# A state-space scan on one core: six of 24 products with B move to ScalarE, and all exponentials go to SBUF

## The chip, the core and the metric

The kernel runs on one core of a Trainium2 chip. The metric is device time in microseconds (us) of one execution, as the median of several runs. A profiled execution gives the trace from which every duration below comes. Engines are named as the profile names them: PE is TensorE (PEld its weight loads), DVE VectorE, ACT ScalarE, POOL GpSimd, SP SyncE, which issues the DMAs.

## What is computed

The kernel computes a small network of four layers. Only layer 0 is touched by the change. It is two Mamba blocks one after the other on a tensor of 4 batches, 96 channels and 4096 tokens, then a mix of channels and a batch normalization. One block, cut to what matters (a state of 16 numbers is kept for each of 192 inner channels):

```
h = layernorm(seq); xs, z = split(h @ in_w)          # 192 channels each
xc = silu(causal convolution of xs with 4 taps + conv_b)
dt, Bm, Cm = split(xc @ xproj_w)                      # 6, 16 and 16 columns
delta = softplus(dt @ dt_w + dt_b)
dA  = exp(delta[..., None] * A)                       # channels x 16 states
dBx = delta[..., None] * Bm[:, :, None, :] * xc[..., None]
state[t] = dA[t] * state[t-1] + dBx[t]
y = sum over states of state[t] * Cm[t] + Dp * xc
out = (y * silu(z)) @ out_w
```

The remaining layers (a convolution block, a linear attention, two feed-forward blocks in 8-bit floats and a mix by Fourier transforms) follow from about 2540 us.

## The kernel before

**Items and tiles.** The tokens of a batch are cut into four sections of T = 1024. An item is one section of one batch in one of the two blocks: 4 x 4 x 2 = 32 items, done one after the other, four batches between two sections of the same batch. An item has 192 channels x 16 states = 3072 rows of tokens, laid out as 24 tiles of 128 partitions x 1024 tokens. A tile is (p, g, j): p is a third of the channels (64), j a half of that third (32), g a group of four states; the partitions are 4 states x 32 channels. The tiles of an item stand in `order`, and the whole program is written out by hand in steps: step m is tile m % 24 of item m // 24, and each engine's queue holds its instructions in the order in which the steps issue them. A *slot* is a step counted from an item's own start.

**The work of one tile.** The exponential dA = exp(delta x A) is made on ScalarE (`exp`, L488) from delta, which was copied to all four state groups of partitions by DMA (`ddb`). The product u = (delta x xc) x B needs B's row on each state's 32 partitions. For 14 of the 24 tiles TensorE spreads B into PSUM with a selecting matrix (`rep`, L474, one for both halves j where they share it), and VectorE multiplies it with `udb` (delta x xc, also copied by DMA) (L523). For the other ten (`pool_tiles`) GpSimd multiplies `udb` by `brep`, B's rows copied by DMA (`times_b`, L509 for two tiles at once, L511 for one). VectorE then scans the 1024 tokens (`scan`, L529). GpSimd multiplies two scanned tiles by C (`times_c`, L534, 128 x 2048), in place in `hs`. TensorE adds up the states (`sum_y`, L551) into a PSUM bank `y`, which starts with Dp x xc (`start_y`, L544). VectorE multiplies by silu(z) (`gate`, L562).

**Where operands lie.** For VectorE's tiles dA is `da` in SBUF and u is in PSUM; the incoming state is put into the first column of `da` by ScalarE (`enter`, L497), and the scan starts from 1.0. For GpSimd's tiles dA is `dap` in PSUM (tag u) and u is `up` in SBUF; the scan takes the state by a pointer. [...] `AHEAD` = 3 is how many tiles ahead an exponential is made and the number of `da` buffers; `hs` has five buffers.

**The first stage.** The steps of an item's preparation (`first_stage`) run up to two items ahead of its scans, each at a given slot (`at_slot`): load x, the layer norm (L282 to L329, with `nt` in the tag up2), the four-tap convolution (`spread`, L215), silu with its table loads (L350), x-projection (L229), softplus (L377), delta and delta x xc to HBM (`spread_out`) and back to all partitions (`load_d`, `load_u`), B and C rows (`load_b`, `load_c`). ScalarE copies most results out of PSUM (L339, L369). Before the first item `prepare` makes the weights; there the convolution taps come by a DMA that broadcasts one row to 97 partitions (L167) and are multiplied with the input weights on VectorE (L184).

Of the kernel before, what the change touches and what calls it, by code (L numbers as in the profile page):

```python
# [9 lines left out]
F32 = mybir.dt.float32  # L10
# [40 lines left out]
class Net:  # L51
# [43 lines left out]
    def layer0(self, dram, scratch):  # L95
        tc, nc, ins = self.tc, self.nc, self.ins
        x_in = ins["x"]
        with ExitStack() as ctx:
# [3 lines left out]
            psum_y = ctx.enter_context(tc.tile_pool(name="l0y", bufs=2, space=PSUM))  # L102
# [44 lines left out]
            AHEAD = 3  # L147
# [3 lines left out]
            def load_weights():  # L151
                for name, shape in (
                    ("sel_r", [128, 32]),
                    ("sel_b", [64, 4, 128]),
# [8 lines left out]
            def prepare():  # L163
                with tc.tile_pool(name="l0s", bufs=1) as wk, tc.tile_pool(name="l0g", bufs=1) as sums_pool:
                    in_w = load(wk, "in_w", [C, 2, HID])
                    rows = wk.tile([C + 1, 2, 4, DIN], F32, name="conv_taps")
                    nc.sync.dma_start(rows, ins["conv_rows"].partition_broadcast(C + 1))  # L167
# [5 lines left out]
                    nc.vector.tensor_scalar_mul(nega, nega, -1.0)  # L173

# [14 lines left out]

                    layer(0)  # L190

                    for m in sorted(stages[0])[:4]:
                        for f in stages[0].pop(m):
                            f()
                    layer(1)
# [14 lines left out]
            def spread(ws, rhs, p):  # L210

                ps = tile_ps(128)
# [48 lines left out]
            def first_stage(k):  # L261
# [16 lines left out]
                @at_slot(-9)  # L278
# [11 lines left out]
                @at_slot(-8)  # L290
                def _():
                    if k:
                        nt = wk.tile([128, 2, T + 1], F32, name="nt", tag="up2")[:, 0]
                    else:
                        nt = first_pool.tile([128, 8 * C], F32, name="nt")
# [12 lines left out]
                @at_slot(-7)  # L308
# [5 lines left out]
                @at_slot(-6)  # L314
# [7 lines left out]
                @at_slot(-5)  # L322
# [10 lines left out]
                def parts_of(name, ws, rhs, slots, bufs):  # L333
# [7 lines left out]
                    for p, (t, out) in enumerate(slots):  # L341
                        at_slot(t)(lambda p=p: m.update({(name, p): spread(ws, rhs, p)}))
                        at_slot(out)(lambda p=p: into(p, m[name, p]))


                parts_of("xc", [(w_x[:, i, k], k) for k in range(4)], n, ((-4, -2), (-3, 0), (-1, 1)), 2)

                @at_slot(2)
# [25 lines left out]

                @at_slot(9)
                def _():
                    nc.scalar.activation(m["delta"], m["delta"], AF.Softplus)  # L377
                    exp_set()
# [18 lines left out]
                parts_of("z", [(w_z[:, i], 3)], n, ((12, 13), (12, 13), (13, 14)), 2)  # L397

                for p in range(3):
                    for j in range(2):  # L400
                        at_slot((15, 23, 31)[p] + j)(lambda p=p, j=j: load_d(m, p, j))
                    at_slot((16 if k else 15, 23, 31)[p])(lambda p=p: load_u(m, p))
                for g, t in ((0, 21), (1, 24), (3, 25), (2, 27)):
                    at_slot(t)(lambda g=g: load_c(m, g))
                at_slot(17 if k else 6)(lambda: load_b(m, 3))
                at_slot(22)(lambda: load_b(m, 2))
# [40 lines left out]
            outer = [(0, 0), (0, 1), (3, 0), (1, 0), (1, 1), (3, 1), (2, 0), (2, 1)]  # L447
            inner = [(0, 0), (3, 0), (0, 1), (3, 1), (1, 0), (2, 0), (1, 1), (2, 1)]
            order = [(p, g, j) for p, eight in enumerate((outer, inner, outer)) for g, j in eight]
            pool_tiles = (2, 5, 7, 9, 11, 13, 15, 18, 21, 23)  # L450
            group_starts = (0, 3, 6, 8, 10, 12, 14, 16, 19, 22)
            ends = {max(t for t, x in enumerate(order) if x[:2] == (p, g)): (p, g) for p in range(3) for g in range(4)}
            sums = {5: (0, 0), 8: (0, 1), 9: (0, 3), 12: (0, 2), 14: (1, 0), 16: (1, 3)}
            sums |= {18: (1, 1), 19: (1, 2), 23: (2, 0), 24: (2, 1), 26: (2, 3), 27: (2, 2)}
            starts = {3: 0, 13: 1, 17: 2}
            gates = {13: 0, 21: 1, 29: 2}
            NTL = len(order)
            last = len(items) * NTL

            def on_pool(m):  # L460
                return m % NTL in pool_tiles
# [5 lines left out]
            def rep(m):  # L467

                k, t = divmod(m, NTL)
                x = psum_x.tile([128, T], F32, name="rep", tag="x")  # L470

                for q, at in enumerate(halves):
                    rows = slice(32 * q, 32 * q + 32)
                    nc.tensor.matmul(  # L474
                        x[:, at], sel_b[rows, order[t][1]], made[k]["dbl"][rows, at], start=True, stop=True
# [1057 lines left out]
```

## Time and profile before

| what | value |
|---|---|
| device time, median of 3 runs | 3846.45 us (3835.75 to 3846.96) |
| the profiled execution's own time | 3837.67 us |
| its span, first to last instruction | 3835.5 us |
| first scan of layer 0 starts, last ends | 78.9 and 2527.7 us |
| scans / products with B on DVE / on POOL, in tiles of an item | 24 / 14 / 10 |
| scan L529 (da, rep) and (dap, state, up), mean | 2288 and 2325 ns |
| product L523 on DVE, mean | 1214 ns |
| products on POOL: with C L534, with B L509 | 4186 and 4533 ns |
| exponential L488 on ACT, mean | 1115 (to PSUM), 1144 ns (to SBUF) |

How to read the views: the busy share counts time in which an engine executes, averaged over the span; 40 slices show it over time in tenths. A group's line gives line, engine, operation, out<-in with shapes, count, then busy us, mean ns of one, and the idle time in front of it with the engine that ended it. A timeline's row gives start, duration, engine, line, operation and count; consecutive instructions overlap a little, so costs in a row are best taken from start to start.

### The profile page before, as it was taken

The page shows a single profiled execution, that of the slowest core. Times are in us where ns is not written, and L with a number is a line of the kernel's source. Part 1 is how long each engine was busy: PE and PEld are TensorE (multiplying, and loading weights), DVE is VectorE, ACT ScalarE, POOL GpSimd, SP SyncE. Part 2 cuts the span into 40 slices and gives each one's busy share as a digit, 9 for nine tenths or more (in the row PEclk, how much of TensorE's full clock was granted, in tenths as well). Part 3 has the DMA queues.
Part 4 walks back from the last instruction along what each step waited for, and adds up shares of the span by engine and source line. Part 5 has one row for each costly group of instructions (what it writes and reads, how often), then busy time and mean ns, then how long its engine had stood idle before and what let it go on. Part 6 is the DMA issues. An engine that isn't in the chain of part 4 may idle for free. (4 is left out here: it accounts for less than half of the span.)

```text
span 3835.5 us, 43134 instructions
## 1 busy us (share of the span) xinstructions
PE 3238.0 (84%) x13656; PEld 1305.1 (34%) x13656; DVE 3036.5 (79%) x2704; ACT 2387.5 (62%) x4640; POOL 2836.6 (74%) x922
## 2 busy tenths in 40 slices
PE   6888888888888888888888888756799998999888
PEld 2222222222222222222222222126544534766643
DVE  4999999999999899999999999962573384444649
ACT  4666676666667666776666666541345686656557
POOL 1999999999999999999999999932001064444527
PEclk9888888887888778887878778757899999999989
DMA  7656666666676566666666666556200000011101
GB/s 182 167 154 165 165 165 165 165 161 154 165 172 164 145 165 163 160 157 165 157 154 169 161 158 163 151 135 211 77 1 1 1 1 6 18 37 35 36 9 58
DMA packets 177867, 463.82 MB, mean 121 GB/s; under 512 B 50804, under 2 KB 52734, under 8 KB 174304
## 3 DMA queue, kind: packets, MB, share of 16 engines
q1 hardware_dynamic: 177640, 461.08, 47.3%
q8 instruction: 108, 1.77, 0.2%
q14 instruction: 119, 0.97, 0.1%
HBM read 387.40 MB, written 73.50 MB: 120 GB/s over the span
## 5 line engine op out<-in xcount | busy, mean ns | idle before, releaser
L534 POOL TENSOR_TENSOR hs<-hs,crep 128x2048 f32<-128x2048 f32 x384 | 1595.8, 4186 | 30.8 <-DVE hs L529 27.0
L474 PE MATMUL rep<-dbl,sel_b 32*128 32x512 f32 x1280 | 458.7, 794 | 365.6 <-DVE hs L529 364.4
L529 DVE TENSOR_TENSOR_SCAN hs<-da,rep 128x1024 f32<-128x1024 f32 x320 | 732.1, 2288 | 35.1 <-ACT da L488 0.7
L488 ACT ACTIVATE dap<-ddb,nega 128x1024 f32<-128x1024 f32 x320 | 356.9, 1115 | 491.8 <-DVE hs L529 490.9
L509 POOL TENSOR_TENSOR up<-udb,brep 128x2048 f32<-128x2048 f32 x128 | 580.3, 4533 | 84.0 <-DMA ddb<-dd 82.8
L488 ACT ACTIVATE da<-ddb,nega 128x1024 f32<-128x1024 f32 x448 | 512.4, 1144 | 76.6 <-DVE hs L529 71.9
L529 DVE TENSOR_TENSOR_SCAN hs<-dap,state,up 128x1024 f32<-128x1024 f32 x240 | 558.1, 2325 | 0.0
L551 PE MATMUL y<-hs,sel_r 128*32 128x512 f32 x3072 | 522.5, 768 | 16.8 <-POOL hs L534 16.7
L523 DVE TENSOR_TENSOR rep<-udb,rep 128x1024 f32<-128x1024 f32 x320 | 388.5, 1214 | 71.2 <-PE rep L474 71.1
L215 PE MATMUL ps<-n,w_x 97*64 97x512 f32 x1536 | 367.2, 621 | 0.0
L474 PEld LDWEIGHTS rep<-dbl,sel_b 32*128 32x128 f32 x1280 | 120.5, 218 | 672.9 <-issue 547.4
L529 DVE TENSOR_TENSOR_SCAN hs<-da,u 128x1024 f32<-128x1024 f32 x128 | 293.0, 2289 | 12.6 <-DVE u L523 0.5
L1091 POOL CAST hq<-y 128x1536 fp8e5<-128x1536 f16 x64 | 93.9, 1467 | 218.8 <-issue 122.6
L215 PEld LDWEIGHTS ps<-n,w_x 97*64 97x64 f32 x1536 | 110.6, 141 | 254.8 <-issue 196.7
L551 PEld LDWEIGHTS y<-hs,sel_r 128*32 128x32 f32 x3072 | 71.9, 122 | 359.9 <-issue 266.9
L529 DVE TENSOR_TENSOR_SCAN hs<-dap,up 128x1024 f32<-128x1024 f32 x80 | 181.3, 2266 | 1.8 <-ACT dap L488 1.7
L523 DVE TENSOR_TENSOR u<-udb,rep 128x1024 f32<-128x1024 f32 x128 | 157.4, 1229 | 25.4 <-DMA udb<-ud 11.9
L965 POOL MEMSET h<- 1x4096 f32 x1 | 3.5, 3506 | 212.9 <-DVE n L871 212.9
L1230 POOL TENSOR_TENSOR av<-av,ec 128x780 f32<-128x780 f32 x32 | 58.7, 1836 | 133.7 <-ACT av L1227 133.7
L511 POOL TENSOR_TENSOR up<-udb,brep 128x1024 f32<-128x1024 f32 x64 | 151.6, 2369 | 0.0
L544 PE MATMUL y<-xc,dp 128*128 128x512 f32 x192 | 140.6, 821 | 0.0
L1203 POOL TENSOR_TENSOR f<-p,p 128x390 f32<-128x390 f32 x64 | 65.1, 1038 | 95.0 <-DVE p L1195 95.0
(260 smaller groups left out, 5962.0 us busy)
## 6 DMA issues: line engine op xcount, KB each, us to landing
ddb<-dd SPq DMA_DIRECT2D x768, 128.0 KB
udb<-ud SPq DMA_DIRECT2D x768, 128.0 KB
crep<-cd SPq DMA_DIRECT2D x512, 128.0 KB
brep<-cd SPq DMA_DIRECT2D x256, 128.0 KB
dd<-delta SPq DMA_DIRECT2D x64, 384.0 KB
band<-in_band SPq DMA_DIRECT2D x24, 1024.0 KB
ud<-delta SPq DMA_DIRECT2D x62, 384.0 KB
x<-in_x SPq DMA_DIRECT2D x32, 384.0 KB
```

The lines of the kernel that those rows point to most:

```text
L215: nc.tensor.matmul(ps[rows], w[:, 64 * p : 64 * p + 64], rhs[:, at.start + shift : at.stop + shift], start=k == 0, stop=k == len(ws) - 1, ...
L474: nc.tensor.matmul(x[:, at], sel_b[rows, order[t][1]], made[k]["dbl"][rows, at], start=True, stop=True)
L488: nc.scalar.activation(da, made[k]["dd", h, j], AF.Exp, scale=nega[:, col : col + 1])
L509: nc.gpsimd.tensor_mul(up, u, twice(made[k]["brep", g]))
L511: nc.gpsimd.tensor_mul(up[:, js[0]], u[:, js[0]], made[k]["brep", g])
L523: nc.vector.tensor_mul(u, made[k]["ud", h][:, j], x)
L529: nc.vector.tensor_tensor_scan(hs[:, 1:], made[k].pop(("da", t)), u, st, ALU.mult, ALU.add)
L534: nc.gpsimd.tensor_mul(hs[:, :, :T], hs[:, :, 1:], twice(made[k]["crep", g]))
L544: nc.tensor.matmul(y, dp[:, items[k][2], p], made[k]["xc"][:, p], start=True, stop=True)
L551: nc.tensor.matmul(made[k]["y", p][row : row + 32], sel_r, made[k]["hs", p, g][:, j, at], start=False, stop=True, skip_group_check=True,)
L1091: nc.gpsimd.tensor_copy(q, y2, saturate=False)
L1203: nc.gpsimd.tensor_add(f[i][:, r], pp[0][:, :, r, :], pp[1][:, :, 1 - r, :])
```

## The change

In layer 0, of an item's 24 products with B, VectorE does 12 (groups g = 0 and 1), GpSimd 6 (`GP` = 2) and ScalarE 6 (`GA` = 3). For ScalarE's six, tokens lie on partitions: TensorE transposes B (`tb`, slot 8) and delta x xc (`turn_du`, slots 15 to 17) into a y bank, ScalarE copies both out (`bt`, `keep_du`), multiplies each of 8 blocks of 128 tokens by each of 4 states' B, which is now a scale per partition (`weigh`, 32 instructions of 128 x 192, slots 19 to 28), and TensorE transposes the result into PSUM, eight transposes a tile (`fill`). Every exponential is written to `da` in SBUF, four ahead with four buffers; `enter` is gone, and every scan takes its state by a pointer. The tiles stand in pairs of the same p and g. PSUM tags x and u are filled in turn. `hs` has four buffers and serves `nt` too; the two y banks have tags of their own and take a third of z, and the transposes of du and B. Slots move by one or so. In `prepare`, the taps come as one row and are spread by three matmuls. The diff, cut to its core:

```diff
-            AHEAD = 3
+            AHEAD = 4
+            GP, GA = 2, 3
...
-                    rows = wk.tile([C + 1, 2, 4, DIN], F32, name="conv_taps")
-                    nc.sync.dma_start(rows, ins["conv_rows"].partition_broadcast(C + 1))
+                    row = load(wk, "conv_rows", [1, 2 * 4 * DIN])
...
+                    def spread_taps(q):
+                        at = slice(q * MB, (q + 1) * MB)
+                        ps = wide(C + 1, MB, q)
+                        nc.tensor.matmul(ps, one, row[:, at], start=True, stop=True)
+                        nc.vector.tensor_copy(taps[:, at], ps)
...
+            def y_bank(k):
+                return psum_y.tile([128, MB], F32, name="y", tag=f"y{k % 2}")
...
-                        nt = wk.tile([128, 2, T + 1], F32, name="nt", tag="up2")[:, 0]
+                        nt = wk.tile([128, 2, T + 1], F32, name="hs", tag="hs", bufs=4)[:, 0]
...
+                @at_slot(8)
+                def _():
+                    m["tb"] = y_bank(3 * k - 2)[:, : 8 * 2 * NST].rearrange("p (q s) -> p q s", q=8)
+                    for q in range(8):
+                        nc.tensor.transpose(
+                            m["tb"][:, q], dbl[: 2 * NST, q * 128 : q * 128 + 128], self.ident[: 2 * NST, : 2 * NST]
+                        )
...
+                    m["bt"] = cp.tile([128, 8, 4], F32, name="bt", tag="bt", bufs=2)
+                    nc.scalar.copy(m["bt"], m["tb"][:, :, 4 * GA : 4 * GA + 4])
...
-                parts_of("z", [(w_z[:, i], 3)], n, ((12, 13), (12, 13), (13, 14)), 2)
+                parts_of("z", [(w_z[:, i], 3)], n, ((12, 13), (12, 13), (14, 15)), 2, 3 * k - 3)
+
+                def turn_du(p):
+                    ps = m["ut", p] = y_bank(3 * k - 3)
+                    for a in range(4):
+                        at = slice(a * 128, a * 128 + 128)
+                        nc.tensor.transpose(ps[:, at], m["du"][:, p, at], self.ident)
...
+                for p in range(3):
+                    at_slot(16 + p)(lambda p=p: keep_du(p))
+                    at_slot(15 + p)(lambda p=p: turn_du(p))
+
+                def weigh(of):
...
+                    for e in of:
+                        q, s4 = divmod(e, 4)
+                        nc.scalar.mul(
+                            m["uta"][:, q, :, 32 * s4 : 32 * s4 + 32].rearrange("t (p j) d -> t p j d", p=3),
+                            m["udt"][:, :, q].rearrange("t p (j d) -> t p j d", j=2),
+                            m["bt"][:, q, s4 : s4 + 1],
+                        )
+
+                e = 0
+                for t, count in ((19, 4), (20, 2), (21, 2), (22, 5), (23, 5), (24, 5), (26, 1), (27, 2), (28, 6)):
+                    at_slot(t)(lambda of=range(e, e + count): weigh(of))
+                    e += count
...
-            outer = [(0, 0), (0, 1), (3, 0), (1, 0), (1, 1), (3, 1), (2, 0), (2, 1)]
-            inner = [(0, 0), (3, 0), (0, 1), (3, 1), (1, 0), (2, 0), (1, 1), (2, 1)]
-            order = [(p, g, j) for p, eight in enumerate((outer, inner, outer)) for g, j in eight]
-            pool_tiles = (2, 5, 7, 9, 11, 13, 15, 18, 21, 23)
+            order = [(p, g, j) for p, gs in enumerate(((0, 2, 1, 3), (0, 2, 3, 1), (3, 0, 2, 1))) for g in gs for j in range(2)]
+            fills = {3: 4, 5: 6, 6: 7, 7: 8, 10: 12, 11: 13, 13: 14, 15: 16, 16: 17, 17: 18, 19: 22, 23: 24}
...
+            def fill(m):
...
+                tag = "xu"[len(filled) % 2]
+                x = psum_x.tile([128, T], F32, name="rep", tag=tag)
+                filled[m] = x, tag
+                if g == GA:
+                    for q in range(8):
+                        nc.tensor.transpose(x[:, q * 128 : q * 128 + 128], made[k]["uta"][:, q, 2 * h + j], self.ident)
+                    return
...
-                if on_pool(m):
-                    da = psum_x.tile([128, T], F32, name="dap", tag="u")
-                else:
-                    da = wk.tile([128, T], F32, name="da", tag="da", bufs=AHEAD)
-                made[k]["da", t] = da
+                da = made[k]["da", t] = wk.tile([128, T], F32, name="da", tag="da", bufs=AHEAD)
                 nc.scalar.activation(da, made[k]["dd", h, j], AF.Exp, scale=nega[:, col : col + 1])
-
-            def enter(m):
...
-                    nc.scalar.mul(a0, a0, state[:, b, i, col : col + 1])
...
+                up = made[k]["up", p] = wk.tile([128, 2, T], F32, name="up", tag="up")
+                nc.gpsimd.tensor_mul(up, made[k]["ud", p], twice(made[k]["brep", GP]))
...
+                if g == GP:
+                    u = made[k]["up", h][:, j]
+                elif g == GA:
+                    u, _ = filled[m]
                 else:
 
-                    u = x if on_pool(m + 1) else psum_x.tile([128, T], F32, name="u", tag="u")
+                    x, tag = filled[m - j]
+                    u = x if j else psum_x.tile([128, T], F32, name="u", tag="u" if tag == "x" else "x")
                     nc.vector.tensor_mul(u, made[k]["ud", h][:, j], x)
...
-                st = 0.0 if s == 0 else state[:, b, i, col : col + 1] if on_pool(m) else 1.0
+                st = state[:, b, i, col : col + 1] if s else 0.0
                 nc.vector.tensor_tensor_scan(hs[:, 1:], made[k].pop(("da", t)), u, st, ALU.mult, ALU.add)
...
-            b_slots = {3: [(0, 1, 3, (0, 1))], 4: [(0, 0, 2, (1,))], 9: [(0, 1, 2, (0, 1))], 13: [(0, 2, 3, (0, 1))]}
-            b_slots[20] = [(0, 2, 2, (1,)), (1, 0, 3, (0, 1))]
+            b_slots = {5: (0, 1), 15: (0, 2), 23: (1, 0)}
```

## The prediction

> **What bounds the kernel now.** I read the page's busy shares and its 40 slices first, then the groups, then the timelines of single engines in layer 0. The last chain on the page lies in the later layers, which the change leaves alone; I don't use it.
>
> ```profile
> PE 3238.0 (84%) x13656; PEld 1305.1 (34%) x13656; DVE 3036.5 (79%) x2704; ACT 2387.5 (62%) x4640; POOL 2836.6 (74%) x922
> ...
> DVE  4999999999999899999999999962573384444649
> ACT  4666676666667666776666666541345686656557
> POOL 1999999999999999999999999932001064444527
> ```
>
> Layer 0 is the first 26 slices. In it VectorE and GpSimd both stand at 9, ScalarE at 6. The groups' view puts the first scan at 78.9 us and the last at 2525.4 (ending 2527.7), for 32 items: 2448.8/32 = 76.5 us an item.
>
> ```profile
> core 0: us, PE busy (x) PEld busy (x) DVE busy (x) ACT busy (x) POOL busy (x), PEclk, DMA share, GB/s
> 1000.00:1400.00 400.00, 343.72 (x1390) 101.44 (x1388) 380.24 (x216) 277.07 (x542) 396.23 (x101) 0.82 0.65 161
> ```
>
> In the middle of layer 0 GpSimd is busy 99%, VectorE 95%, TensorE 86%, ScalarE 69%. So two engines bound it together.
>
> ```profile
> L534 POOL TENSOR_TENSOR hs<-hs,crep 128x2048 f32<-128x2048 f32 x384 | 1595.8, 4186 | 30.8 <-DVE hs L529 27.0
> ...
> L529 DVE TENSOR_TENSOR_SCAN hs<-da,rep 128x1024 f32<-128x1024 f32 x320 | 732.1, 2288 | 35.1 <-ACT da L488 0.7
> ...
> L529 DVE TENSOR_TENSOR_SCAN hs<-dap,state,up 128x1024 f32<-128x1024 f32 x240 | 558.1, 2325 | 0.0
> ...
> L523 DVE TENSOR_TENSOR rep<-udb,rep 128x1024 f32<-128x1024 f32 x320 | 388.5, 1214 | 71.2 <-PE rep L474 71.1
> ```
>
> The operands matter. A scan reads either da (SBUF) and rep or u (PSUM), or dap (PSUM) and up (SBUF); a product reads udb (SBUF) and rep (PSUM). No large VectorE instruction of layer 0 has two SBUF inputs (the one L394 of the first item apart).
>
> ```profile
> 1500.88 2.29 DVE L529 TENSOR_TENSOR_SCAN hs<-da,rep 128x1024 f32<-128x1024 f32 x1
> 1503.09 2.33 DVE L529 TENSOR_TENSOR_SCAN hs<-dap,state,up 128x1024 f32<-128x1024 f32 x1
> 1505.50 1.23 DVE L523 TENSOR_TENSOR u<-udb,rep 128x1024 f32<-128x1024 f32 x1
> 1506.84 2.29 DVE L529 TENSOR_TENSOR_SCAN hs<-da,u 128x1024 f32<-128x1024 f32 x1
> ```
>
> From start to start: scan 2.20 us, scan with a state pointer 2.24 (2.41 where the next product waits for its bank), product 1.33, gate 0.6. An item is 14x2.20 + 10x2.24 + 14x1.33 + 3x0.6 = 73.6 us; the rest of the 76.5 is waiting, most of it for rep: 71.1+1.7 us in all, 2.3 an item.
>
> [...] a later layer has such a pair:
>
> ```profile
> 3559.08 0.55 DVE L1242 SCALAR_TENSOR_TENSOR zz<-av 128x384 f32<-128x384 f32 x1
> ...
> 3559.30 2.43 POOL L1203 TENSOR_TENSOR f<-p,p 128x390 f32<-128x390 f32 x2 [3.44 <-DVE p L1195]
> 3559.54 0.85 DVE L1245 SCALAR_TENSOR_TENSOR z<-av 128x6 f32<-128x6 f32 x1
> ...
> 3560.32 0.55 DVE L1242 SCALAR_TENSOR_TENSOR zz<-av 128x384 f32<-128x384 f32 x1
> 3560.78 0.98 DVE L1245 SCALAR_TENSOR_TENSOR z<-av 128x6 f32<-128x6 f32 x1
> ```
>
> L1245 handles 6 elements and takes 0.15 us alone; here 0.85 and 0.98, each ending just as a GpSimd product (about 0.93) ends. The two GpSimd instructions take 2.43 together instead of 1.86. With both queued, the two engines alternate.
>
> [...] here eight transposes at L318 take 1.30 us, 0.16 each[...].
>
> **The change, part by part (an item, layer 0).**
>
> *VectorE's own work.* Two products fewer: -2x1.33 = -2.7. All scans take the state by pointer: 14x0.04 x 3/4 of the items = +0.4. Net -2.3.
>
> *Exponentials in SBUF.* Six scans an item (B group 2, tiles 2, 3, 10, 11, 20, 21) now read da and up, both in SBUF. The trace has no such scan; I bound it. Below: nothing[...]. Above: a full GpSimd instruction ahead of every one of the six, 6x4.15 = 25. I take the alternation shown above. In VectorE's queue the two scans of a pair follow one another; in GpSimd's the product with C of the pair before (L534, 4.15 from start to start) becomes ready when the scan before this pair ends. So the first scan issues at once, that product waits for it (2.24), runs, and the second scan waits for the product: 4.15 for each of three pairs, 12.4 us. Is GpSimd free when the first scan comes? Its work is 12x4.15 + 3x4.49 + 3.40 = 66.7, and 6x2.24 = 13.4 of being shut out makes 80.1; below the period that comes out, so mostly yes. Behind the waiting scan stand all later scans and products; behind them ScalarE's exponentials (four ahead) and TensorE's fills.
>
> *GpSimd.* It loses one pair and two single products with B: 4.5+2x2.35 = 9.2. In the program before that would count; now it hides behind VectorE.
>
> *ScalarE.* 32 weighings of 192 elements. Eight at L312 with 96 elements take 1.80 us from start to start, 0.225 each[...] I take 0.31: 9.9 us, with three copies of 512 at 0.49 (start to start in ScalarE's timeline) and a small one, 11.5. Away go 14 one-element products (L497, 0.19) in three quarters of the items, 2.0. ScalarE rises from some 53 (69% of 76.5) to 62 us, hidden beside VectorE's 88, and still if VectorE stood at its own 72.
>
> *TensorE.* Six fills become eight transposes each; ten broadcasts become six: 6x(1.3 to 1.7) - 4x1.1; twelve transposes of du 1.9, eight of B 0.8: about +7, to 72 us. Hidden in sum, not in order. Where a new wait sits: at slot 15 the first transpose of du needs the y bank that ScalarE's copy of z empties, and that copy stands behind the exponential which needs scan 15's buffer. After scan 15: 1.05 + 0.49 + 0.65 for the transposes + 1.5 for tile 17's fill + about 0.2 of signals = 3.9, while scan 16 covers 2.24: VectorE waits 1.7. The next fill stands behind a transpose that needs the copy at slot 16, which has the squares of the norm (2.4) and an exponential before it: another 1.6. Together 3.3, of which I count as new only what exceeds the 2.3 waited for rep before, which the earlier fills can remove: +1.0, between 0 and +3.3.
>
> *Moved.* The norm's nt takes a turn of hs, whose buffers go from five to four; at four, scan 16 waits for the product with C of tiles 10 and 11; VectorE's tiles 12 to 15 lie between (2x2.24 + 2x3.57 = 11.6), and GpSimd needs 3.4+4.15. I count nothing; without that cover it would be the difference. Loads of brep fall from eight issues to four on SP's queue; C loads move by one to three slots; they have 10 us and more.
>
> *Start.* VectorE waits there for the broadcast of the conv taps:
>
> ```profile
> 29.92 1.15 DVE L184 TENSOR_TENSOR w_x<-w_ps,conv_taps 97x192 f32<-97x192 f32 x4 [23.46 <-DMA conv_taps<-in_conv_rows]
> ```
>
> One row and three matmuls take its place. in_w lands at about 9; two spreads[...] and copies (0.7) put L184 at 13 to 14: 16 earlier. About 2 to 3 us of ScalarE's copies and weighings now stand before the first exponential (76.4). I take -14, between -8 and -18.
>
> **Sum.** 76.5 - 2.3 + 12.4 + 1.0 = 87.6 us an item, 11.1 more; 32 items: +355; start -14: +341. The profiled execution took 3837.7 us (span 3835.5): 4179. The median of the runs, 3846.5, lies 9 above it, so I say 4185.
>
> **Rivals.**
> - *The scan doesn't contend* (other side). For it: [...] the proof above is of another instruction. Then 76.5 - 2.3 + (0 to 3.3, likely 1.5) = 75.7: 32x(-0.8) - 14 = -40, 3800. The sign turns once contention costs more than 40/32 = 1.25 us an item, 0.4 a pair.
> - [...] Then only GpSimd suffers and becomes the bound with 80.1: 3.6x32 - 14 = +101, 3940. Against it: L1245 let GpSimd in after L1242.
> - *GpSimd takes two turns.* At 3372.05 L1242 took 2.73, waiting for three GpSimd instructions queued in a row. If the first scan of a pair waits too (a rest of 0 to 4, say 1.2 a pair): 91.2, +14.7x32 - 14 = +456, 4295.
>
> **How the numbers follow.** Alternation 0.60, GpSimd's two turns 0.12, VectorE keeps it 0.10, no contention 0.18. The range must leave out no more than the last: 3930 to 4310. What a measurement of this kernel can tell from no change is about 0.3%, 11.5 us. The three contention cases are slower (0.82); the fourth ends faster at 0.13, within 0.3% at 0.03, slower at 0.02.
>
> **What would show it.** Right: the second scan of each hs<-da,state,up pair recorded at about 6.4 us and the first near 2.3, so a mean near 4.4; other scans at 2.29 to 2.33; GpSimd idle some per cent with its products before such scans stretched by 2.2; 87 to 88 us an item; DVE waiting at tiles 17 and 18 for rep; L184's successor near 14 us. Wrong: if those scans all last 2.3 us, or if GpSimd's products stretch and the scans don't.

## The result and the profile after

The changed kernel takes 4518.2 us (median of 4 runs, 4514.3 to 4520.0), the kernel before 3843.1 us beside it: ratio 1.176, 95% interval 1.174 to 1.178. The profiled execution took 4519.4 us, its span is 4517.5. My 4185 us (3930 to 4310) had the sign and half the size.

The page of the changed kernel, busy shares and slices:

```profile
PE 3503.4 (78%) x15326; PEld 1600.2 (35%) x15326; DVE 3312.6 (73%) x2644; ACT 2751.2 (61%) x5456; POOL 2683.0 (59%) x826
...
DVE  6878887787888888888888778888616538444549
ACT  6666666665666666666666656665414467666548
POOL 2777777676677767777776767777320006444427
```

Before, VectorE and GpSimd stood at 9 in layer 0. Now no engine does: VectorE 8, GpSimd 7, TensorE 7, ScalarE 6. The stretch that the prediction reads, 1000 to 1400 us, has now:

```profile
1000.00:1400.00 400.00, 302.04 (x1280) 115.93 (x1278) 327.07 (x158) 252.72 (x497) 285.16 (x66) 0.78 0.47 120
```

TensorE fell from 86 to 76%, VectorE from 95 to 82, ScalarE from 69 to 63, GpSimd from 99 to 71. A kernel that became slower while all four engines became less busy is waiting on itself. The page's groups, VectorE's scans and products and GpSimd's product with C (time | busy us, mean ns | idle before, and its releaser):

```profile
L580 POOL TENSOR_TENSOR hs<-hs,crep 128x2048 f32<-128x2048 f32 x384 | 1725.8, 4499 | 673.8 <-DVE hs L575 576.8
...
L575 DVE TENSOR_TENSOR_SCAN hs<-da,state,up 128x1024 f32<-128x1024 f32 x144 | 576.5, 4045 | 37.7 <-PE y L597 37.7
...
L569 DVE TENSOR_TENSOR u<-udb,rep 128x1024 f32<-128x1024 f32 x192 | 234.1, 1219 | 150.6 <-PE rep L539 121.4
...
L575 DVE TENSOR_TENSOR_SCAN hs<-da,up 128x1024 f32<-128x1024 f32 x48 | 186.1, 3915 | 13.7 <-PE y L597 13.2
```

The scans with two SBUF inputs last 4.0 us on the mean, all others 2.28 to 2.35. That is the contention with GpSimd's products that I forecast. But GpSimd, which I had nearly full, idles 673.8 us before L580, mostly waiting for scans. VectorE waits 260.2 us in all for a buffer of hs that TensorE's sum L597 empties, and 56.6 for one that the norm's transposes L336 empty; before the change all its waits in layer 0 came to some 2.9 us an item (76.5 - 73.6).

The first scan starts at 63.6 us (78.9 before), the last at 3202.4: (3202.4 - 63.6)/32 = 98.1 us an item against 76.5. So 32 x 21.6 = 691 us come from the loop, -15 from the start, +5 from the layers after it, together the 682 by which the span grew.

To see where, I took from VectorE's timeline the time from the start of each scan to the start of the next (mean of items 8 to 27), and set beside it what the same instructions take without a wait: 2.26 us for a scan, 1.32 more for a product between, 0.6 for a gate. "Scan 16" is the scan of tile 16, and the gap after tile 15 ends where it starts. An item without any wait is 71.8 us.

```
gap after tile     3     6     7     9    10    11    13    15    16    17    21   item
without a wait   3.58  2.26  3.58  2.26  2.24  2.26  4.17  2.26  2.26  3.58  3.58  71.8
changed kernel   7.41  3.64  4.65  3.90  4.85  3.19  4.93  8.46  2.26  8.16  7.46  98.8
```

(Over all 32 items it is 98.1.) Tiles 2 and 3, 10 and 11, 20 and 21 are the pairs with two SBUF inputs: 3.8 + 2.6 + 3.9 = 10.3 us of contention. The remaining 98.1 - 71.8 - 10.3 = 16.0 us are waits. VectorE's idle gaps between the first scan and the last, those over 0.15 us added up, come to 16.0 us an item too. Two thirds of these lie at tiles 16 and 18: 6.1 us (hs for scan 16), 2.7 us (rep for product 18) and 1.9 us (hs for scan 18). VectorE's timeline from scan 15 on:

```profile
1504.21 2.35 DVE L575 TENSOR_TENSOR_SCAN hs<-da,state,rep 128x1024 f32<-128x1024 f32 x1
1512.50 4.59 DVE L575 TENSOR_TENSOR_SCAN hs<-da,state,rep 128x1024 f32<-128x1024 f32 x2 [5.94 <-PE y L597]
1519.82 1.23 DVE L569 TENSOR_TENSOR u<-udb,rep 128x1024 f32<-128x1024 f32 x1 [2.73 <-PE rep L539]
1522.94 2.35 DVE L575 TENSOR_TENSOR_SCAN hs<-da,state,u 128x1024 f32<-128x1024 f32 x1 [1.89 <-PE ps L336]
...
1528.71 8.45 DVE L575 TENSOR_TENSOR_SCAN hs<-da,state,up 128x1024 f32<-128x1024 f32 x2
```

TensorE's timeline of the same stretch:

```profile
1508.36 1.09 PE L432 MATMUL y<-ident,delta 128*128 128x128 f32 x4 [4.23 <-ACT z L357]
1509.24 1.91 PE L534 MATMUL rep<-ident,uta 128*128 128x128 f32 x8
1511.08 1.24 PE L597 MATMUL y<-hs,sel_r 128*32 128x512 f32 x8
```

And ScalarE's:

```profile
1506.59 1.15 ACT L546 ACTIVATE da<-ddb,nega 128x1024 f32<-128x1024 f32 x1 [2.34 <-DVE hs L575]
1507.64 0.57 ACT L357 COPY z<-y 128x512 f32<-128x512 f32 x1
```

Read from the bottom up. Scan 15 ends at 1506.56 and frees a da buffer; ScalarE starts the exponential that waited for it, and only then copies z out of its bank (1507.64). TensorE's first transpose of du needs that bank and has stood still for 4.23 us; behind it in TensorE's queue stand the fill of tile 17 and the sum of (1,2), the pair p = 1, g = 2 of tiles 10 and 11. Scan 16 needs (1,2)'s hs buffer, so it starts when that sum is done, at 1512.50. VectorE thus waits for a chain that VectorE's own scan 15 started.

The last line of VectorE's timeline is a contended pair: 8.45 us for two scans, with no idle time and no releaser. GpSimd at that moment:

```profile
1528.96 6.05 POOL L580 TENSOR_TENSOR hs<-hs,crep 128x2048 f32<-128x2048 f32 x1 [7.26 <-DVE hs L575]
```

The product starts just after the first scan and lasts 6.05 us in place of some 4.2; the second scan ends 2.15 us after the product, about one scan. On both engines the wait is recorded as duration.

### The profile page after: what moved, and what is told of

The parts are those of the page before. It is cut to its first block, busy times and chain, and to the rows that moved or that the text cites. A ratio compares the mean times of both kernels' runs of the same rounds, so it can differ in the third digit from the quotient of the medians.

```text
span 4517.5 us, 46762 instructions
## 1 busy us (share of the span) xinstructions
PE 3503.4 (78%) x15326; PEld 1600.2 (35%) x15326; DVE 3312.6 (73%) x2644; ACT 2751.2 (61%) x5456; POOL 2683.0 (59%) x826
## 5 line engine op out<-in xcount | busy, mean ns | idle before, releaser
L580 POOL TENSOR_TENSOR hs<-hs,crep 128x2048 f32<-128x2048 f32 x384 | 1725.8, 4499 | 673.8 <-DVE hs L575 576.8
L546 ACT ACTIVATE da<-ddb,nega 128x1024 f32<-128x1024 f32 x768 | 884.4, 1152 | 1015.6 <-DVE hs L575 988.4
L575 DVE TENSOR_TENSOR_SCAN hs<-da,state,rep 128x1024 f32<-128x1024 f32 x288 | 670.3, 2342 | 202.5 <-PE y L597 153.9
L575 DVE TENSOR_TENSOR_SCAN hs<-da,state,up 128x1024 f32<-128x1024 f32 x144 | 576.5, 4045 | 37.7 <-PE y L597 37.7
L597 PE MATMUL y<-hs,sel_r 128*32 128x512 f32 x3072 | 493.1, 727 | 26.2 <-POOL hs L580 26.2
L534 PE MATMUL rep<-ident,uta 128*128 128x128 f32 x1536 | 302.2, 349 | 164.8 <-DVE hs L575 114.1
L451 ACT ACTIVATE uta<-delta,bt 128x192 f32<-128x192 f32 x1024 | 382.7, 442 | 0.0
L575 DVE TENSOR_TENSOR_SCAN hs<-da,state,u 128x1024 f32<-128x1024 f32 x144 | 338.1, 2348 | 57.1 <-PE ps L336 41.5
L534 PEld LDWEIGHTS rep<-ident,uta 128*128 128x128 f32 x1536 | 231.2, 178 | 338.0 <-DVE hs L575 148.3
L539 PE MATMUL rep<-dbl,sel_b 32*128 32x512 f32 x768 | 252.1, 736 | 96.2 <-DVE hs L575 96.2
L432 PE MATMUL y<-ident,delta 128*128 128x128 f32 x372 | 101.4, 427 | 268.6 <-ACT delta L437 138.1
L575 DVE TENSOR_TENSOR_SCAN hs<-da,rep 128x1024 f32<-128x1024 f32 x96 | 217.7, 2282 | 81.5 <-PE y L597 55.4
L575 DVE TENSOR_TENSOR_SCAN hs<-da,up 128x1024 f32<-128x1024 f32 x48 | 186.1, 3915 | 13.7 <-PE y L597 13.2
L432 PEld LDWEIGHTS y<-ident,delta 128*128 128x128 f32 x372 | 65.5, 214 | 359.5 <-ACT delta L437 221.7
```

The lines of the kernel that those rows point to most:

```text
L432: nc.tensor.transpose(ps[:, at], m["du"][:, p, at], self.ident)
L451: nc.scalar.mul(m["uta"][:, q, :, 32 * s4 : 32 * s4 + 32].rearrange("t (p j) d -> t p j d", p=3), m["udt"][:, :, q].rearrange("t p (j d) - ...
L534: nc.tensor.transpose(x[:, q * 128 : q * 128 + 128], made[k]["uta"][:, q, 2 * h + j], self.ident)
L539: nc.tensor.matmul(x[:, at], sel_b[rows, g], made[k]["dbl"][rows, at], start=True, stop=True)
L546: nc.scalar.activation(da, made[k]["dd", h, j], AF.Exp, scale=nega[:, col : col + 1])
L575: nc.vector.tensor_tensor_scan(hs[:, 1:], made[k].pop(("da", t)), u, st, ALU.mult, ALU.add)
```

## The experiments

Theory: two costs, independent in kind. (1) Scans with two SBUF inputs, which last 4.0 us on the mean in place of 2.3 as they and GpSimd's products wait for each other, about 10 us an item. (2) TensorE's queue in program order, in which a matmul that waits for ScalarE holds up fills and sums that were ready, passed on to VectorE by hs's four buffers. Rivals: all of it is contention; ScalarE or TensorE simply has too much work; the two costs are one.

The kernel before, run again beside them, took 3834 to 3837 us (medians). "item" is the time from the first scan's start to the last's, over 32.

```
kernel       median us   ratio to before, 95%      item us
a_nt           4306.5    1.123  (1.122 to 1.125)    91.5
a_hs5          4301.4    1.122  (1.119 to 1.125)    91.4
a_order        4403.6    1.150  (1.147 to 1.153)    94.6
a_port         4296.6    1.121  (1.119 to 1.124)    91.3
a_da           4267.5    1.113  (1.112 to 1.115)    90.5
a_nt_port      4141.6    1.080  (1.078 to 1.082)    86.4
a_best1        3962.9    1.034  (1.031 to 1.037)    81.1
a_best2        3888.2    1.014  (1.011 to 1.016)    78.6
a_best3        3784.4    0.986  (0.984 to 0.988)    75.2
a_best3s       4107.9    1.070  (1.069 to 1.072)    85.6
b_sbuf         4437.9    1.159  (1.154 to 1.163)    95.1
b_start        3817.9    0.995  (0.994 to 0.997)    76.4
b_proj         3856.7    1.006  (1.004 to 1.009)    77.9
b_delta2       3816.7    0.995  (0.993 to 0.996)    76.3
```

### hs's buffers: a_nt, a_hs5

```diff
-  nt = wk.tile([128, 2, T + 1], F32, name="hs", tag="hs", bufs=4)[:, 0]
+  made[k - 1]["udb"] = wk.tile([128, 2, T + 1], F32, name="udb", tag="udb", bufs=2)
+  nt = made[k - 1]["udb"][:, 0]        # and load_u of that pair in slot 18, not 17
```

> The changed kernel, with one edit: the norm's transposed tile nt takes no turn of hs any more; it lies in the udb buffer of the pair that is loaded next (free between the last product of tile 15 and that load, which goes from slot 17 to 18). Nothing is left out. Theory (the loop over hs's four buffers and TensorE's queue at slots 15 to 18 is the part that I sized at +1.0 and counts some 10 us an item): the scan of tile 16 then needs the buffer of (1,0), summed at slot 13, and no longer that of (1,2), summed at slot 16 behind the first transposes of du; VectorE's waits for hs (260.2 + 56.6 us in the changed kernel) nearly vanish: 317/32 = 9.9 us an item less, 98.2 - 9.9 = 88.3, 4518 - 317 = 4200 us. Rival A (those waits only stand in for a ScalarE or TensorE that is too slow in slots 15 to 20): they turn into waits for rep at tiles 17 and 18, at least half is given back, 4350 to 4500 us. Rival B ([...] contention at more places than I thought): 4518 us, no change.

4306.5, -212 us where I expected -317. The wait before scan 16 is gone (gap after tile 15: 2.26). 2.4 us of it come back one tile later: the fill of tile 17 still stands behind the transpose of du, and scan 17 waits for it. The gap after 17 falls to 4.22. A third of what the theory expected is given back, at tile 17 as rival A said, but the whole is below its 4350. So the turn of hs is a real part, and the queue's order stays behind it.

```diff
-  tag="hs", bufs=4)
+  tag="hs", bufs=5)     # the second layer uses the first one's w_x, w_z, dp, dtw
```

> The changed kernel, with one edit: five buffers of hs, as before the change, nt still among their turns. The room for the fifth comes from keeping the first layer's input, delta and skip weights alone and using them for the second layer too (part of the computation is changed; the instructions of the loop stay the same). Theory (the step of my prediction that counted the fifth buffer at nothing): scan 16 then needs the buffer of (1,0), as in a_nt, and scans 10 and 12 no longer wait for sums either (1.6 and 0.8 us an item in the changed kernel), so it is at or below a_nt: 4240 to 4310 us. What stays is the fill of tile 17 behind the first transposes of du (2.4 us in a_nt). Rival (what a_nt removed was something else about nt, its place in the queues, and not the turn): above 4400 us.

4301.4, as forecast beside a_nt, and with the same 2.4 us before scan 17. Scans 10 and 12 no longer wait for sums (scan 12 now waits 0.75 us for a fill). This is the very item of the change that my prediction had counted at nothing: undoing it alone gives 217 us. It also shows the contention as I had predicted it: with no wait ahead of scan 10, all three pairs have a first scan of 2.3 us and a second of 6.1 to 6.2.

### TensorE's queue: a_order

```diff
-  at_slot(16 + p)(lambda p=p: keep_du(p))
-  at_slot(15 + p)(lambda p=p: turn_du(p))
+  at_slot(17 + p)(lambda p=p: keep_du(p))
+  at_slot(16 + p)(lambda p=p: turn_du(p))
```

> The changed kernel, with one edit: the three transposes of du and the copies behind them come one slot later (16 to 18 and 17 to 19 in place of 15 to 17 and 16 to 18), so that in TensorE's queue the fills of tiles 17 and 18 and the sum of (1,2) stand ahead of them. Nothing is left out; nt still takes a turn of hs. Theory (TensorE's queue stands still behind a transpose that waits for a copy on ScalarE, and hs's four buffers hand that on to the scan of tile 16): the gaps after tiles 15 and 17, 8.5 and 8.2 us in the changed kernel against 2.3 and 3.6 without a wait, fall by some 8 us together: 4518 - 260 = 4260 us. Rival A (four buffers with nt among them are too few whatever TensorE's order): above 4450 us. Rival B (ScalarE is late in slots 15 to 18, not TensorE's order): the waits move to rep at tiles 17 and 18, above 4400 us.

4403.6, between theory and rival A. Rival B's number (above 4400) fits, but its wait for rep doesn't come. The wait for hs before scan 16 halves (6.1 to 3.2 us an item) and that for rep before product 18 vanishes (2.7 to 0), but scan 18's wait for the buffer that nt holds grows from 1.9 to 4.0. With nt among four buffers, order alone doesn't do it; with nt out, order is what is left. The two edits work on one loop from two ends.

### Two SBUF inputs: a_port, a_nt_port, a_da, b_sbuf

```diff
-  u = made[k]["up", h][:, j]
+  u, _ = filled[m - j - 2]
```

> The changed kernel, with one edit: the six scans of B group 2 read as second input the PSUM tile that the pair before them used, and not GpSimd's product up, which is still computed; their results are therefore another sequence (part of the computation is changed). They then have one SBUF input. Theory (each pair's second scan waits for one GpSimd product): 48 of hs<-da,state,up were 1.7 us longer than the others on average over both of a pair, (4.04 - 2.33) x 6 = 10.3 us an item; all scans last 2.29 to 2.35 us, 4518 - 330 = 4190 us, while the waits for hs at tiles 16 and 18 stay. Rival A (the waits at hs and rep cover what is saved): 4350 us or more. Rival B (GpSimd's product with B is what is late[...]): the scans last the same.

4296.6: all scans last 2.29 to 2.35 us, so what made the long ones long is up as a second input in SBUF. Rival B, that up came late, isn't ruled out by this run, which doesn't read up; a_da, below, rules it out. But only 222 us come back of the 330 that the records held: the waits at scan 16 and 18 stay as they were (6.4 and 1.9), and others appear or grow, 1.2 us before scan 6, and 1.9 before scan 12 where it was 0.8. VectorE's idle gaps come to 18.9 us an item, 2.9 more than in the changed kernel; that contention had given TensorE this time is the likely reason.

> Both edits at once: nt in the next udb buffer, and the six scans of B group 2 reading a PSUM tile in place of up (part of the computation is changed). Theory (two independent costs): the savings add, 4518 - 317 - 330 = 3870 us, some 78 us an item. Rival (the two hide each other: once one is gone, the other's waits shrink or grow): 50 us or more off that sum to either side.

4141.6, not 3870: the rival holds. 12.5 us of waits an item sit at tiles 6, 7, 10, 12, 14, 17 and 18, all for TensorE's fills and sums. Taking two waits away uncovered others of the same kind at other tiles.

```diff
+  if order[m % NTL][1:] == (GP, 1):      # in exp, two tiles ahead and not four
+      da = psum_x.tile([128, T], F32, name="dap", tag=filled[m - 3][1])
```

> The changed kernel, with one edit: of each pair of B group 2, the exponential of the second tile goes into the free PSUM bank pair of the pair before, two tiles ahead in place of four. Nothing is left out. So the first scan of a pair still has two SBUF inputs, and the second has one. Theory (alternation: the first scan issues at once, one product with C slips in, the second waits for it): the second lasts 2.35 us, GpSimd's product waits 2.2 us for the first and hides that; 10.3 us an item less, 4190 us, the same as with no contention at all. Rival ([...] GpSimd is often in the middle of a product when the first scan issues): the first scan now waits up to 4.15 us, 4300 to 4500 us.

4267.5, a little better than with no contention at all in a_port; the theory's mechanism is right (the second scans still read up and last 2.32 us, so up wasn't late), its size was short as in a_port: the idle gaps grew to 18.3 us an item.

```diff
   da = made[k].pop(("da", t))
+  if on_pool(m):
+      da = made[k]["dd", h, j]
```

> The kernel before, with one edit: its ten scans an item with up read as first input the rows of delta in SBUF (ddb) and not their exponential in PSUM, which is still computed; their results are another sequence (part of the computation is changed). So they have two SBUF inputs, and nothing else of the change is there. Theory (such a scan and GpSimd's products take turns): GpSimd is busy 99% there, so each of the ten scans meets a product; a scan waits for the rest of one, between 2.1 us on the mean and 4.15, and GpSimd is shut out for 2.24 us ten times an item, so the item is at least 76 + 22 = 98 us: 3840 + 32 x 22 = 4550 us at the least, up to 4900. Rival (what was long in the changed kernel is something else about its scans, such as GpSimd's product being late): 3840 us.

4437.9: in the kernel before, with nothing else of the change, two SBUF inputs make a scan longer. From the groups of b_sbuf between 60 and 3000 us:

```profile
L532 DVE TENSOR_TENSOR_SCAN hs<-ddb,state,up 128x1024 f32<-128x1024 f32 x227 | 929.2, 4093 | 37.1 <-POOL up L511 26.3 <-POOL up L509 10.7
```

4.09 us against 2.33 with dap: 1.76 x 10 = 17.6 us an item, of 18.7 that the item grew. I expected at least 2.1 each; the floor I set was too high: the scans of tiles 7 and 13 last 6.2 us on the mean, but those of tiles 9 and 11 2.7.

### Putting the queues in order: a_best1, a_best2, a_best3

a_best1 is a_nt, a_da and a_order together with:

```diff
-  if at == 32: project(k0)
-  if at == 33: project_z(k0)
+  if at == 33: project(k0); project_z(k0)
-  ((19, 4), (20, 2), (21, 2), (22, 5), (23, 5), (24, 5), (26, 1), (27, 2), (28, 6))
+  ((19, 5), (20, 5), (21, 5), (22, 6), (23, 6), (24, 5))
-  (18 if k else 15, 25, 31)
+  (18 if k else 15, 24, 31)
```

> [...] Nothing is left out. Six edits: the second exponential of each B group 2 pair into PSUM; nt in the next udb buffer; the transposes of du one slot later; the projection's matmuls with x from slot 32 to 33, behind the fill and the sum that they held up while they waited for a copy of delta; all weighings done by slot 24, ahead of the Silu block; one load of udb a slot earlier. Theory (the change's excess is contention plus queue order, and nothing else): VectorE's own 72 to 73 us an item remain, with some 3 us of waits: 76 us, 32 x (76 - 98.1) = -707: 3810 us. Rival (TensorE, at a granted clock of 0.85 and busy some 70 us an item with the transposes, is the bound once the order is right): 82 us or more, above 4000 us.

3962.9, short of 3810 and better than the rival's 4000. The waits at 6, 7, 10, 12, 16 and 17 are gone. Two large things are left: 3.4 us before product 14, whose fill stands behind the matmuls of z, and 4.0 at tile 20, where the one scan of the pair that still has two SBUF inputs meets a product in 28 of 32 items. In 12 of them it waits for a second product as well, one that started after the scan. VectorE's and GpSimd's timelines of the longest:

```profile
2403.29 9.97 DVE L587 TENSOR_TENSOR_SCAN hs<-da,state,up 128x1024 f32<-128x1024 f32 x1
2398.68 12.44 POOL L592 TENSOR_TENSOR hs<-hs,crep 128x2048 f32<-128x2048 f32 x3
```

The scan comes 0.5 us after the second of three products has started, and ends at 2413.26, 2.1 us after the third. So GpSimd can take two turns while a scan waits. Why it does so here, and in other items doesn't, no run shows.

```diff
-  fills = {3: 4, 5: 6, 6: 7, 7: 8, 10: 12, 11: 13, 13: 14, 15: 16, 16: 17, 17: 18, 19: 22, 23: 24}
+  fills = {2: 4, 5: 6, 6: 7, 7: 8, 10: 12, 11: 13, 12: 14, 14: 16, 15: 17, 16: 18, 20: 22, 22: 24}
-  if order[m % NTL][1:] == (GP, 1):
+  if order[m % NTL][1] == GP:            # the first tile's into the pair's other tag
-  @at_slot(11)    # the product du
+  @at_slot(13 if k else 11)
```

> The changed kernel with the edits of a_best1 and three more: both exponentials of a B group 2 pair in PSUM (the two bank pairs of the pair before), each fill issued as soon as its bank pair is free (tiles 4, 14, 16, 17, 18 and 24 one slot earlier, 22 one later), and the product du two slots later, so that GpSimd doesn't stand still behind the transfer of delta. Nothing is left out. Theory (of a_best1's 81.1 us an item 4.0 are the first scan at tile 20 meeting a product of GpSimd, 3.4 the fill of tile 14 behind the matmuls of z, about 2 other fills): 81.1 - 7.5 = 73.6 us, 32 x -7.5 = -240: 3720 us. Rival (TensorE and its clock are the bound by then): 3850 us or more.

3888.2, far above the theory's 3720 and where the rival, TensorE as the bound, had it (3850 or more). But VectorE waits for single fills and sums, which a_best3 then removes by edits of order, and TensorE itself stands idle in front of one of them (2.95 us below): it isn't full, so the rival's number held and its cause did not. Both waits named are gone, and two took their place. TensorE's timeline of a_best2 shows the first:

```profile
1033.94 1.10 PE L627 MATMUL ps<-x,ident 96*96 96x512 f32 x2
1037.99 2.02 PE L627 MATMUL ps<-x,ident 96*96 96x512 f32 x2 [2.95 <-ACT delta L360]
1039.94 4.48 PE L247 MATMUL ps<-z,out_w 64*96 64x512 f32 x12
1044.35 1.09 PE L539 MATMUL rep<-ident,uta 128*128 128x128 f32 x8
1045.38 1.06 PE L609 MATMUL y<-hs,sel_r 128*32 128x512 f32 x8
```

The projection needs the bank that ScalarE's copy of delta empties, that copy stands behind an exponential that waits for scan 8, and the sum of (0,1), which frees scan 12's buffer, is last in the row: 3.2 us an item. It is the loop of slot 15 again with other names. The second, 2.6 us at tile 22, is a fill behind a convolution.

```diff
-  delta: ((6, 7), (6, 7), (7, 8))        xc: ((-5, -4), (-3, -2), (-1, 0))
+  delta: ((6, 7), (6, 7), (7, 7))        xc: ((-4, -3), (-2, -1), (-1, 0))
-  sums 10: (0, 1)
+  sums  9: (0, 1)
```

> The changed kernel with the edits of a_best2 and three more: delta's last copy in slot 7, ahead of an exponential that waits, so that the projection doesn't stand still; the sum of (0,1) a slot earlier; the first two convolutions of the next item one slot later, behind the fill of tile 22. Nothing is left out. Theory (a_best2's 78.6 us an item hold 3.2 before the scan of tile 12, which waits for that sum, and 2.6 at tile 22, whose fill stands behind a convolution, and next to nothing else): 73 to 75 us an item, 32 x -4.6 = -147, some 3740 us, below the kernel before. Rival (TensorE is full[...]; waits come up elsewhere): 3830 us or more.

3784.4, 44 above the theory's 3740, and faster than the kernel before by 1.4% (1.2 to 1.6). Some 16 of these 51 us are the start. Its 75.2 us an item hold 2.7 us of waits. So moving six products to ScalarE and TensorE was sound, and their added work was indeed hidden; putting the exponentials of group 2 in SBUF was not, and a_best3 has them in PSUM again (a_best3s, below, prices that). What cost some 680 us was where the new instructions stood, and where their operands lay.

### Contention alone: a_best3s

```diff
-  return order[m % NTL][1] == GP
+  return False
```

> a_best3 with one edit: the exponentials of B group 2 go into SBUF again, as in the changed kernel. Nothing is left out. Theory (contention alone costs what the changed kernel's records show, 10.3 us an item): 3784 + 330 = 4115 us, an item of 85.5 us; the second scan of a pair lasts 6.2 us. My prediction's term, 12.4, would give 4180 us. Rival (with waits gone GpSimd is nearer to its limit, 67 + 13 us an item, so first scans meet a product too): 4200 us or more. Rival (waits elsewhere took it back in the changed kernel and do so here): 3784 + 165 to 222, 3950 to 4005 us.

4107.9, +323 us: 10.1 us an item by time, as the theory said (4115), and neither rival. The groups of a_best3s agree, (4.07 - 2.33) x 6 = 10.4:

```profile
L587 DVE TENSOR_TENSOR_SCAN hs<-da,state,up 128x1024 f32<-128x1024 f32 x144 | 580.5, 4072 | 40.9 <-PE y L609 40.7
```

Which scan of a pair pays wasn't as expected: the second at tile 11 (6.2 us), but the first at tile 2 (5.0 on the mean), and at tiles 20 and 21 now one, now the other. This is close to the kernel that my prediction described: exponentials in SBUF, and queues that hardly wait. It takes 85.6 us an item where I had 87.6.

### The kernel before: b_start, b_proj, b_delta2

The edit of b_start is the change's own start (the row of taps, `spread_taps`) in the kernel before.

> The kernel before with only the change's start: one row of conv taps spread to the partitions by matmuls in place of the broadcast by DMA. Nothing is left out. Theory (the start is worth what the first scan's place says, 78.9 to 63.6 us in the changed kernel, and is independent of the rest): -15 us, 3840 to 3825 us. Rival (VectorE catches up that lead later, or other loads are late instead): 3835 to 3840 us.

3817.9, 0.995 (0.994 to 0.997): the start is worth 16 to 18 us by itself.

```diff
-  if at == 32: project(k0)
+  if at == 33: project(k0)               # b_start, just ahead of project_z
```

> The kernel before with the change's start and with the projection's two matmuls with x from slot 32 to slot 33, behind the broadcast for tile 10. Nothing is left out. Theory (in the kernel before, too, VectorE's one steady wait, 2.2 us an item at tile 10, is TensorE's queue standing behind those matmuls, which wait for ScalarE's copy of delta): 15 + 32 x 2 = 80 us less, 3840 to 3760 us. Rival (TensorE is simply late there at its lower clock): as with the start alone, 3825 us.

3856.7, slower: the wait at tile 10 is gone, but 3.5 us now come before product 12, whose fill stands behind both parts of the projection.

```diff
-  delta: ((6, 7), (6, 7), (7, 8))
+  delta: ((6, 7), (6, 7), (7, 7))        # b_start and this
```

> The kernel before with the change's start and with delta's last copy in slot 7 in place of 8, ahead of the exponential that waits for the scan of tile 8. Nothing is left out. Theory (VectorE's wait of 1.8 us an item at tile 10 is TensorE's queue behind the projection, which waits for that copy): b_start's 3818 less 32 x 1.8 = 58: 3760 us. Rival (TensorE is late there because of its lower clock): 3818 us.

3816.7, as b_start: the rival holds. The table by stretches of b_delta2 shows why; from one item's scan 9 to scan 10 (us, busy time of each engine, granted clock, DMA share, GB/s):

```profile
925.90:933.20 7.30, 7.30 (x19) 1.68 (x19) 3.65 (x4) 7.24 (x11) 7.30 (x2) 0.50 0.25 51
```

TensorE is busy all of the 7.3 us, at half its clock, and doesn't wait for the copy. The 32 items of the kernel before say the same: this stretch takes 3.4 to 3.6 us in the six that had the full clock throughout, and 6.9 to 7.2 in the twelve that had half of it. In the kernel before, this wait is a matter of TensorE's speed; in the changed one, where TensorE stood idle 4.2 us ahead of L432, the wait at tile 16 is one of its order.

## Why the prediction was half right

*VectorE's own work, -2.3.* It is 71.8 us where I had 73.6 - 2.3 = 71.3; right to 0.5.

*Contention, +12.4.* Right in kind, 10.3 in the changed kernel and 10.1 to 10.4 alone. The second scans of tiles 3 and 21 last 6.1 to 6.2 us, as I said, the first 2.3; 6.2 us is one scan (2.3) and nearly one product (4.2). The pair at tile 10 went otherwise: there GpSimd was in the middle of a product, the first scan waited (4.6 us on the mean) and the second mostly didn't (2.55). In the changed kernel each pair pays at most once, and the pair at tile 10 less, for the rest of a product. Of the rivals, "the scan doesn't contend" and "VectorE keeps it" (both scans of a pair go ahead of GpSimd's product) are ruled out by these records and by b_sbuf. "GpSimd takes two turns" isn't the changed kernel's case, where no scan lasted over 6.22 us and no pair paid twice; but a_best1 has it at tile 20, so the alternation that I assumed is not a rule.

*Start, -14.* L195, the successor of L184's line in the kernel before, starts at 17.0 and not at 14, 13 us earlier and not 16 (the copies of the three spreads start 1.70 us apart, at 12.09, 13.79 and 15.50), and yet the first scan comes 15.3 us earlier; b_start gives 16 to 18. The size came out, its steps didn't: luck in part, and what gained the rest isn't shown.

*ScalarE and TensorE, hidden in sum.* True: a_best3 does all of it in 75.2 us an item, with ScalarE busy 62 us of them, as I had summed. A weighing takes 0.35 us from start to start in the changed kernel (five in a row 1.84, one alone 0.44 to 0.45); my 0.31 was an estimate. Eight transposes in a row take 1.09 us at full clock, a fill by two matmuls 1.13, so replacing one by the other cost nothing.

*The step that failed: "+1.0, between 0 and +3.3", with "Moved. ... I count nothing".* Waits in the changed kernel are 16.0 us an item, not 2.9 + 1.0: +13.1 where I had +1.0. I had found the chain at slot 15 and its length, 3.9 us (of which "about 0.2 of signals" was an estimate; in the stretch above the exponential starts 0.03 us after scan 15's end, and the first transpose 0.15 after z's copy), and set scan 16 against it as cover. But scan 16 waits for the end of that same chain. I had named the right buffer (tiles 10 and 11) and looked only at GpSimd's product with C, which was ready in time (done at 1502, and scan 15 ended at 1506.6); the buffer comes free when TensorE's sum of it is done, and that sum stood in slot 16 behind the transpose that I had just found waiting. So the cover was part of the chain. a_hs5 and a_nt price this at 217 and 212 us. Some 5.4 us more stand at tiles 7, 8, 10, 12 and 14, which I hadn't looked for: I went through the queue of the one slot where I saw a new wait, and not through the slots in which old waits met new instructions. Other orders and buffers took nearly all of these away, at 7, 8, 10 and 12 in a_best1 and at 14 in a_best2. No single undoing gave its full share, since other waits came or grew in its place: at tile 17 in a_nt, at tiles 6 and 12 in a_port.

*What stays open* is how much of the 16.0 is order and how much TensorE's clock. At tile 10 of the changed kernel the wait goes with the clock: the gap after tile 9 is 4.5 to 4.6 us in the 19 items with half the clock, and 2.8 or less in the six with all of it. The gap after tile 17 nearly always ran at half. And the two seem to feed each other: in layer 0 of the changed kernel TensorE stands idle for more than 3 us 113 times, and in the 2 us after such a gap the granted clock was 0.50 on the mean (0.79 after gaps of 1 to 2 us); a fill of eight transposes takes 1.09 us at full clock and 1.91 in the timeline above, at 1509, where it was 0.50. a_best3 has five such gaps. So the edits of order may have gained in part by keeping the clock up; no run holds the clock fixed.

With 16.0 put for 3.9 and 10.3 for 12.4, my sum gives 71.8 + 10.3 + 16.0 = 98.1; as both are read from VectorE's records, this is a check, good to some 0.2. No rival of mine had a loop of waits; 4295, the highest, came from contention alone.

## What to carry to other kernels

When a wait is set against an instruction that covers it, ask what releases that instruction, down to its output buffer's last reader: a buffer is free when the last engine in its row has read it (scan 16's here at 1512.50, after TensorE's sum), and that engine's queue may hold the very wait. When buffers go from five to four, walk the rotation turn by turn, temporary tenants (here nt) included, and put beside each turn the slot of its last reader and what stands ahead of that in its queue. A kernel that slows down while every engine becomes less busy is to be read by gaps from instruction to instruction, not by busy shares; and a scan that merely grew longer, with no idle time (6.2 us in place of 2.3), can be a wait too.

## What I had not expected of the hardware

- The wait of a scan with two SBUF inputs for a GpSimd product appears inside the scan's duration (6.2 us for a 2.3 us scan), with no idle time and no releaser; the view of waits doesn't list it.
- Whether the scan or GpSimd's next product goes first isn't fixed: in the changed kernel no scan lasted over 6.22 us, but a scan in a_best1 waited 7.6 us, for the rest of one GpSimd product and the whole of the next.
- TensorE's mean granted clock moves with the kernel though its work is nearly the same: 0.832 in the changed kernel, 0.869 in a_best3s, 0.923 in a_best3 over the whole span. In the changed kernel's trace it was 0.50 on the mean in the 2 us after gaps of over 3 us in TensorE's work (above), and waits go with it: in the kernel before, one that is there in an item with half the clock (7.2 us from scan 9 to 10) is absent in another with all of it (3.6).
